# One relu per block of four groups, sums four groups behind, and a ring of 21 groups in a graph-network kernel

## The chip, the cores and the metric

The kernel runs on one core of one Trainium2 chip. The metric is the device time of one execution in microseconds (us), as the median of several runs; lower is better. A core has five engines that run side by side and meet through semaphores: TensorE (PE in the profile; PEld is its loading of weights), VectorE (DVE), ScalarE (ACT), GpSimd (POOL) and SyncE (SP). Transfers are done by 16 DMA engines; here SyncE issues the plain ones and GpSimd the gathers, one instruction for each 128 rows that are fetched by a list of indices.

## The reference

The task is one layer of a graph network over 12,500 nodes with 96 features and 412,500 edges, sorted by their target node, with 4 features each.

```python
def _mlp(h, W, b, gamma, beta):
    h = jax.nn.relu(h @ W + b)
    mu = jnp.mean(h, axis=0)
    var = jnp.mean(jnp.square(h - mu), axis=0)
    return gamma * (h - mu) * jax.lax.rsqrt(var + EPS) + beta

node_feat = _mlp(x, W_node, b_node, g_node, beta_node)
edge_feat = _mlp(edge_attr, W_edge, b_edge, g_edge, beta_edge)
message = jnp.concatenate([x[row], x[col], edge_feat], axis=1)
message = _mlp(message, W_msg, b_msg, g_msg, beta_msg)
agg = jax.ops.segment_sum(message, col, num_segments=N)
out = _layernorm(x + agg + node_feat)
```

The means and variances of an `_mlp` go over all rows, so over all edges for the messages. Everything is in float32.

## The kernel before

The message of an edge is relu(P[src] + Q[dst] + edge part), where P and Q are products of `x` with two thirds of `W_msg`. The first stages make the tables P and Q (`table`), the nodes' own part (`nodes`), and the statistics of the edges' part (`edge_norm`, L273). They end near 1045 us. Then comes the loop over the edges (`fast`, L327), which ends near 5317 us, and a last stage for the layer norm (L701 on).

**Tiles.** 128 edges make a tile, four tiles a group (512 edges), four groups a block (`BG`). There are 806 groups in 202 blocks. P's rows for a group are gathered by GpSimd, four gathers of 128 rows, into a place of the `ring` (L89), which has `RING` places. The groups of the first 26 blocks (`SPILL`) were gathered in the stages before and laid off in DRAM; SyncE brings such a block back as `pb`. `order` (L357) mixes these 26 blocks evenly among the 176 that are gathered while the loop runs. The first `RING` groups of the latter are gathered ahead of the loop (L353).

**One block.** `load` has SyncE fetch the edges' features and 31 rows of Q for each group. `edges` (L429) multiplies the edge features on TensorE into `pr`. `prepare` (L436) turns `pr` into `left`: ScalarE's relu (L440) for the edge part, and VectorE's comparison (L441) for 31 rows that pick the target node. `linear` (L443) multiplies `left` with `rhs` for one group into `z`, of which there are two buffers, so the product of group k+1 needs the addition of group k-1 to be done. `message` (L451) adds the gathered rows (`hs`, L463, VectorE), which frees the ring's place, and takes the relu into `h` (L465, ScalarE) for two groups at a time. Once per block it also writes an indicator of the target node into `h` (L457, VectorE). `sums` (L471) multiplies `h` with itself and the indicator on TensorE (L480), which gives sums by node and the moments for the statistics, in `pa`. `add` (L483) adds `pa` into `agg` (L493, two instructions) and `gram` (L494) on VectorE.

**Order.** In this loop the order of every engine's instructions is written out by hand: each engine does them in the order of the program. Step k of the loop (L506) issues the product of group k+1, the message of group k, and the sums of group k-2; in a block's first step also `edges` of the next block, in its third `prepare` of the next block; and `add` when `SKEW` steps have passed since the block's first. After the message of a gathered group the gathers for the group `RING` places further on are issued. `h` and `left` have two buffers, `rhs` three.

Of the kernel before, what the change touches and what calls it, by code (L numbers as in the profile page):

```python
# [11 lines left out]
F32 = mybir.dt.float32  # L12
I32 = mybir.dt.int32
AF = mybir.ActivationFunctionType
# [6 lines left out]
N, C, E, ED = 12500, 96, 412500, 4  # L21
EPS = 1e-5
P = 128
# [3 lines left out]
GT, GE, BG = 4, 512, 4  # L27
NT = -(-E // P)
NG = -(-NT // GT)
# [18 lines left out]
WN, WS, WM = 31, 16, 7  # L48
# [1 line left out]
KR = C + WN + 1  # L50

SPILL = 26 * BG
RING = 25
RAW = 3
SKEW = 6
HB, RB = 2, 3
CL, CE = 2, 2
J = 8
# [14 lines left out]
def gnn(ctx, tc, t):  # L73
    nc = tc.nc
# [13 lines left out]
    nc.sync.dma_start(src_raw, t["src"][:, :RAW * BG * GT])  # L88
    ring = rpool.enter_context(tc.tile_pool(name="ring", bufs=RING))  # L89
    xp = xpool.enter_context(tc.tile_pool(name="x", bufs=1)).tile([C, NN], F32, name="xp")  # L90
# [27 lines left out]
    rel = const.tile([P, NGP, GT], F32, name="rel")  # L118
# [71 lines left out]
    for i in range(NS):  # L190
        k, n = Q * i, C - Q * i
# [135 lines left out]
    def fast(ring):  # L327
        def ahead_of(g):
            return gather(g, ring.tile([P, GT, C], F32, name="pg"))

        with tc.manual_schedule(engines={ET.SP, ET.Pool}):
# [6 lines left out]
            for r in range(WM + NN, WT, 64):  # L338
                n = min(64, WT - r)
# [6 lines left out]
            n = 0  # L346
# [4 lines left out]
            for _ in store:  # L351
                pass
            got = {g: ahead_of(g) for g in range(SPILL, SPILL + RING)}  # L353

# [10 lines left out]
        with tc.tile_pool(name="fix", bufs=1) as fix, tc.tile_pool(name="msg", bufs=2) as work, \  # L365
# [12 lines left out]
            for x in hb:  # L378
                nc.vector.memset(x[:, :, :, C:C + 1], 1.0)

            eas, block, prs, zs, pas, pair = {}, {}, {}, {}, {}, [None]

            def load(s):

                b = order[s]
                first = SPILL // BG
                c, o = ((b - first) // CL * CL + first, CL) if b >= first else (b // CE * CE, CE)
                if c not in eas:
                    o = min(o, NBL - c)
                    eas[c] = work.tile([P, o, GE], F32, name="ea" if b >= first else "eae")  # L390
                    for i in range(BG):
                        nc.sync.dma_start(eas[c][Q * i:Q * i + EK, :, :], t["ea"][EK * i:EK * (i + 1), c:c + o, :])
                    nc.sync.dma_start(eas[c][EK:P:Q, :, :], rel_d[:, c * BG * GE:(c + o) * BG * GE]
                                      .rearrange("o (b g e) -> (o g) b e", g=BG, e=GE))
                ea = eas[c][:, b - c, :]
                _, val = nc.values_load_multi_w_load_instructions(
                    base[:, b:b + 1], engines=[ET.SP], min_val=0, max_val=N - 1,
                    skip_runtime_bounds_check_because="they are nodes' numbers")
                rows = q_tab[bass.ds(val[0], WN), :]
                rows = bass.AP(rows.tensor, rows.offset, [[C, WN], [WS * C, BG], [1, C]], None, rows.runtime_checks)  # L400
                nc.sync.dma_start(rhs[C:C + WN, s % RB, :, :], rows)
                block[s] = ea

            def fetch(s):
                b = order[s]
                if b * BG < SPILL:
                    back = work.tile([P, BG, GT, C], F32, name="pb")
                    nc.sync.dma_start(back, spill[b].rearrange("p g (a c) -> p g a c", a=GT))
                    for i in range(BG):
                        got[b * BG + i] = back[:, i, :, :]  # L410
# [18 lines left out]
            def edges(s):  # L429

                prs[s] = ps.tile([P, BG, GE], F32, name="pr", bufs=1)
                for i in range(min(BG, NG - order[s] * BG)):
                    nc.tensor.matmul(prs[s][:C + WN, i, :], we[Q * i:Q * i + EK + 1, :],  # L433
                                     block[s][Q * i:Q * i + EK + 1, :], start=True, stop=True)

            def prepare(s):  # L436

                n = min(BG, NG - order[s] * BG)
                pr, x = prs[s], left[s % 2]
                nc.scalar.activation(x[:C, :n, :], pr[:C, :n, :], AF.Relu)  # L440
                nc.vector.tensor_scalar(x[C:C + WN, :n, :], pr[C:C + WN, :n, :], 0.0, None, op0=OP.is_equal)  # L441

            def linear(k):  # L443
                s, g = steps[k]
                n = min(GT, NT - g * GT)
                zs[k] = ps.tile([P, GT, C], F32, name="z")
                for i in range(n):
                    nc.tensor.matmul(zs[k][:, i, :], left[s % 2][:KR, g % BG, i * P:(i + 1) * P],  # L448
                                     rhs[:KR, s % RB, g % BG, :], start=True, stop=True)

            def message(k):  # L451
                s, g = steps[k]
                n = min(GT, NT - g * GT)
                i = g % BG
                h, z, pg = hb[s % HB], zs.pop(k), got.pop(g)
                if i == 0:
                    nc.vector.tensor_tensor(  # L457
                        h[:, :, :, C + 1:C + 1 + WN], rel[:, g:g + BG, :].unsqueeze(3).to_broadcast([P, BG, GT, WN]),
                        iota.unsqueeze(2).to_broadcast([P, BG, GT, WN]), op=OP.is_equal)
                if i % 2 == 0:  # L460
                    pair[0] = work.tile([P, 2, GT, C], F32, name="hs")
                hs = pair[0]
                nc.vector.tensor_add(hs[:, i % 2, :n, :], z[:, :n, :], pg[:, :n, :])  # L463
                if i % 2 and n == GT:
                    nc.scalar.activation(h[:, i - 1:i + 1, :, :C], hs, AF.Relu)  # L465
                elif i % 2 or g == NG - 1:
                    for o in range(i // 2 * 2, i + 1):
                        m = GT if o < i else n
                        nc.scalar.activation(h[:, o, :m, :C], hs[:, o % 2, :m, :], AF.Relu)

            def sums(k):  # L471

                s, g = steps[k]
                n = min(GT, NT - g * GT)
                h = hb[s % HB][:, g % BG, :, :]
                if g % BG == 0:
                    pas[s] = ps.tile([C + 1, BG, P], F32, name="pa")
                for i in range(n):
                    r = min(P, E - (g * GT + i) * P)
                    nc.tensor.matmul(pas[s][:, g % BG, :C + 1 + WN], h[:r, i, :C + 1], h[:r, i, :C + 1 + WN],  # L480
                                     start=i == 0, stop=i == n - 1)
# [15 lines left out]

            n, ahead = len(steps), SPILL + RING
            with tc.manual_schedule(engines={ET.SP, ET.Pool, ET.PE, ET.DVE, ET.Activation}):
                load(0)  # L500
                fetch(0)
                load(1)
                edges(0)
                prepare(0)
                linear(0)
                for k in range(n + SKEW):  # L506
                    s, g = steps[min(k, n - 1)]
                    if k < n and g % BG == 0:
                        if s + 2 < len(order):
                            load(s + 2)  # L510
                        if s + 1 < len(order):
                            fetch(s + 1)
                    if k + 1 < n:
                        linear(k + 1)
                    if k < n:
                        message(k)
                    if 0 <= k - 2 < n:
                        sums(k - 2)
                    if k < n and s + 1 < len(order):
                        if g % BG == 0:  # L520
                            edges(s + 1)
                        if g % BG == 2:
                            prepare(s + 1)
                        if g % BG == 3 and order[s + 1] < RAW:
                            convert(s + 1)
                    if k >= SKEW and (k - SKEW) % BG == 0:
                        add((k - SKEW) // BG)
                    if k < n and g >= SPILL and ahead < NG:
                        got[ahead] = ahead_of(ahead)
                        ahead += 1  # L530
# [12 lines left out]
    def general():  # L543

        with tc.tile_pool(name="gd", bufs=1, space=DRAM) as gd, tc.tile_pool(name="gfix", bufs=1) as fix, \
# [138 lines left out]
            for b in range(NB):  # L684
# [7 lines left out]
                nc.vector.tensor_copy(agg[:, WM + b * P:WM + (b + 1) * P], px)  # L692

    fast(ring)
    rpool.close()
    bad = nc.values_load(flag, min_val=0, max_val=1, skip_runtime_bounds_check_because="a comparison's result")
# [4 lines left out]
    with tc.tile_pool(name="fin", bufs=2) as work, tc.tile_pool(name="fin_ps", bufs=2, space=PSUM) as ps:  # L701
# [10 lines left out]
        for i in range(0, NB, NBY):  # L712
            n = min(NBY, NB - i)
# [55 lines left out]
```

## Time and profile before

| | |
|---|---|
| median of 3 runs | 5365.72 us (5353.82 to 5367.68) |
| the profiled execution | 5379.39 us, with a span of 5377.6 us |
| loop over groups | about 1045 to 5317 us |
| TensorE, weight load, VectorE, ScalarE, GpSimd busy | 3364.1, 2570.3, 1699.3, 1077.6, 3106.6 us |
| granted TensorE clock, mean of the span | 0.665 of full speed |
| gathers in the loop's ring | 2807, of 959 ns each |
| `hs` addition, relu of two groups, L457, L441 | 555, 843, 666 and 2291 ns each |

A row of a group reads: line, engine, operation, what it writes and reads, and after the bar its time in all and the mean of one in ns. A row of the timeline reads: start and duration in us, engine, line, operation, what it writes and reads, how many were merged, and in brackets how long the engine stood idle before and what ended that. "Issue" stands for time in which the engine waited for nothing that the profile shows, "remote" for a signal whose sender it cannot name. A row of the stretches gives the busy time of each engine, with the number of instructions, the granted TensorE clock as a share of full speed, the share of the DMA engines' time, and GB/s.

### The profile page before, as it was taken

The numbers are of one execution on the slowest core, as the hardware profiler recorded it, in microseconds if no ns is written. First come the engines' busy times: TensorE is split into PE (matmuls) and PEld (weight loads), VectorE is DVE, ScalarE is ACT, GpSimd is POOL, SyncE is SP. The second block draws the span as 40 slices with busy tenths as digits, with TensorE's granted clock in tenths as the row PEclk, the third lists the DMA queues.
The fourth block names the chain that finished last, engine by engine and source line by source line (L and its number), as shares of the span: only waits on it lengthen the run. The fifth ranks groups of instructions, "written<-read, shape, count | busy, mean of one in ns | idle before, by whom it ended". The sixth has DMA issues, their size and how long they took to land. (4 is left out here: it accounts for less than half of the span.)

```text
span 5377.6 us, 46715 instructions
## 1 busy us (share of the span) xinstructions
PE 3364.1 (63%) x16705; PEld 2570.3 (48%) x16705; DVE 1699.3 (32%) x2622; ACT 1077.6 (20%) x1015; POOL 3106.6 (58%) x3244
## 2 busy tenths in 40 slices
PE   5566662666656666665667666656666666666668
PEld 5333330354545545544445554544455545545447
DVE  1445551622222322222222322322232222223225
ACT  0224441411111111111111111111111111111112
POOL 5454456155566656666666666666666666666661
PEclk9755555566666766667676766666766666666667
DMA  5332332111111111111111111111111111111112
GB/s 165 112 97 61 71 68 48 29 33 37 39 44 38 43 42 44 43 38 42 42 43 45 42 38 43 44 42 45 37 43 42 41 45 36 43 43 42 44 37 84
DMA packets 188578, 270.80 MB, mean 50 GB/s; under 512 B 121095, under 2 KB 121480, under 8 KB 187330
## 3 DMA queue, kind: packets, MB, share of 16 engines
q0 software_dynamic: 103136, 158.62, 12.2%
q1 hardware_dynamic: 77120, 98.40, 6.6%
q10 hardware_dynamic: 8080, 10.71, 0.7%
q8 instruction: 133, 2.18, 0.2%
q14 instruction: 109, 0.89, 0.1%
HBM read 225.90 MB, written 41.60 MB: 50 GB/s over the span
## 5 line engine op out<-in xcount | busy, mean ns | idle before, releaser
L162 POOL DMA_INDIRECT pg<-p_tab,src x2807 | 2690.8, 959 | 1767.1 <-DVE hs L463 922.8
L448 PE MATMUL z<-rhs,left 128*128 128x96 f32 x6446 | 1222.7, 339 | 878.3 <-issue 672.8
L448 PEld LDWEIGHTS z<-rhs,left 128*128 128x128 f32 x6446 | 1093.2, 249 | 1183.6 <-issue 903.1
L480 PE MATMUL pa<-h 128*97 128x128 f32 x6446 | 1246.3, 331 | 556.2 <-issue 551.6
L480 PEld LDWEIGHTS pa<-h 128*97 128x97 f32 x6446 | 1015.4, 209 | 654.7 <-issue 653.3
L463 DVE TENSOR_TENSOR hs<-z,pg 128x384 f32<-128x384 f32 x702 | 385.2, 555 | 2599.2 <-remote 1537.6
L465 ACT ACTIVATE h<-hs 128x768 f32<-128x768 f32 x402 | 338.9, 843 | 2867.6 <-DVE hs L463 1846.0
L290 PE MATMUL pr<-ea,wide 10*128 10x512 f32 x1212 | 405.4, 1074 | 285.7 <-issue 177.6
L162 POOL DMA_INDIRECT stage<-p_tab,src x368 | 351.0, 954 | 369.6 <-DMA spill<-stage 240.0
L440 ACT ACTIVATE left<-pr 96x2048 f32<-96x2048 f32 x202 | 377.2, 1867 | 643.6 <-remote 439.7
L441 DVE TENSOR_SCALAR left<-pr 31x2048 f32<-31x2048 f32 x202 | 462.9, 2291 | 108.3 <-ACT left L440 75.5
L296 DVE BATCH_NORM_STATS2 estats<-r 128x6 f32<-128x512 f32 x606 | 365.8, 678 | 326.8 <-issue 191.1
L433 PE MATMUL pr<-ea,we 6*127 6x512 f32 x1404 | 411.1, 808 | 62.6 <-issue 47.5
L290 PEld LDWEIGHTS pr<-ea,wide 10*128 10x128 f32 x1212 | 209.6, 320 | 480.2 <-issue 291.8
L294 ACT ACTIVATE r<-pr 128x1024 f32<-128x1024 f32 x303 | 297.1, 1024 | 458.0 <-remote 290.0
L433 PEld LDWEIGHTS pr<-ea,we 6*127 6x127 f32 x1404 | 117.9, 223 | 206.6 <-issue 190.6
L457 DVE TENSOR_TENSOR h<-rel,iota 128x496 f32<-128x496 f32 x202 | 134.6, 666 | 0.0
L463 DVE TENSOR_TENSOR hs<-z,pb 128x384 f32<-128x384 f32 x104 | 56.6, 554 | 233.1 <-remote 85.2
L150 PE MATMUL pt<-w_msg,xp 96*128 96x96 f32 x392 | 88.7, 421 | 60.4 <-issue 37.1
L493 DVE TENSOR_TENSOR agg<-pa,agg 97x62 f32 x404 | 90.1, 223 | 85.4 <-remote 54.8
L150 PEld LDWEIGHTS pt<-w_msg,xp 96*128 96x128 f32 x392 | 85.5, 330 | 63.4 <-issue 48.6
L494 DVE TENSOR_TENSOR gram<-pa,gram 97x388 f32<-97x388 f32 x202 | 111.4, 551 | 0.1
(107 smaller groups left out, 634.7 us busy)
## 6 DMA issues: line engine op xcount, KB each, us to landing
pg<-p_tab,src POOLq DMA_INDIRECT x2807
spill<-stage SPq DMA_DIRECT2D x26, 768.0 KB
pb<-spill SPq DMA_DIRECT2D x26, 768.0 KB
ea<-in_ea SPq DMA_DIRECT2D x75, 160.0 KB
rhs<-q_tab SPq DMA_DIRECT2D x202, 46.5 KB
ea<-in_ea SPq DMA_DIRECT2D x352, 20.0 KB
stage<-p_tab,src POOLq DMA_INDIRECT x368
q_tab<-trow SPq DMA_DIRECT2D x7, 672.0 KB
```

Of the source, the lines that this page charges most:

```text
L150: nc.tensor.matmul(pt[:, g, :], xp[:, k:k + P], w, start=True, stop=True)
L162: nc.gpsimd.indirect_dma_start(out=pg[:, i, :], out_offset=None, in_=tab[:, :], in_offset=bass.IndirectOffsetOnAxis(ap=idx[:, k:k + 1], ax ...
L290: nc.tensor.matmul(pr[:, k % 2, :], wide[Q * i:Q * i + 2 * EK, :], ea[Q * i:Q * i + 2 * EK, b % J, :], start=True, stop=True)
L294: nc.scalar.activation(r, pr, AF.Relu)
L296: nc.vector.bn_stats(stats[:, (k - o) % NS, (k - o) // NS, :], r[:, 1 - o, :])
L433: nc.tensor.matmul(prs[s][:C + WN, i, :], we[Q * i:Q * i + EK + 1, :], block[s][Q * i:Q * i + EK + 1, :], start=True, stop=True)
L440: nc.scalar.activation(x[:C, :n, :], pr[:C, :n, :], AF.Relu)
L441: nc.vector.tensor_scalar(x[C:C + WN, :n, :], pr[C:C + WN, :n, :], 0.0, None, op0=OP.is_equal)
L448: nc.tensor.matmul(zs[k][:, i, :], left[s % 2][:KR, g % BG, i * P:(i + 1) * P], rhs[:KR, s % RB, g % BG, :], start=True, stop=True)
L463: nc.vector.tensor_add(hs[:, i % 2, :n, :], z[:, :n, :], pg[:, :n, :])
L465: nc.scalar.activation(h[:, i - 1:i + 1, :, :C], hs, AF.Relu)
L480: nc.tensor.matmul(pas[s][:, g % BG, :C + 1 + WN], h[:r, i, :C + 1], h[:r, i, :C + 1 + WN], start=i == 0, stop=i == n - 1)
```

## The change

The relu of a block's four groups becomes one ScalarE instruction, issued after the fourth addition; its buffer `hs` now holds four groups, twice. The sums of a group are issued four steps behind its message in place of two (`BG` for 2), and `add` eight steps after a block's first in place of six. The indicator (L457) is written after the third addition of a block, ahead of the next block's `prepare`, and no longer ahead of the first. The ring has 21 places in place of 25, which gives back the memory that `hs` takes.

```diff
--- before.py
+++ after.py
@@ -50,9 +50,9 @@
 KR = C + WN + 1
 
 SPILL = 26 * BG
-RING = 25
+RING = 21
 RAW = 3
-SKEW = 6
+SKEW = 8
 HB, RB = 2, 3
 CL, CE = 2, 2
 J = 8
@@ -378,7 +378,7 @@
             for x in hb:
                 nc.vector.memset(x[:, :, :, C:C + 1], 1.0)
 
-            eas, block, prs, zs, pas, pair = {}, {}, {}, {}, {}, [None]
+            eas, block, prs, zs, pas, four = {}, {}, {}, {}, {}, [None]
 
             def load(s):
 
@@ -454,19 +454,20 @@
                 i = g % BG
                 h, z, pg = hb[s % HB], zs.pop(k), got.pop(g)
                 if i == 0:
+                    four[0] = work.tile([P, BG, GT, C], F32, name="hs")
+                hs = four[0]
+                nc.vector.tensor_add(hs[:, i, :n, :], z[:, :n, :], pg[:, :n, :])
+                if i == min(2, NG - 1 - (g - i)):
+                    b = g - i
                     nc.vector.tensor_tensor(
-                        h[:, :, :, C + 1:C + 1 + WN], rel[:, g:g + BG, :].unsqueeze(3).to_broadcast([P, BG, GT, WN]),
+                        h[:, :, :, C + 1:C + 1 + WN], rel[:, b:b + BG, :].unsqueeze(3).to_broadcast([P, BG, GT, WN]),
                         iota.unsqueeze(2).to_broadcast([P, BG, GT, WN]), op=OP.is_equal)
-                if i % 2 == 0:
-                    pair[0] = work.tile([P, 2, GT, C], F32, name="hs")
-                hs = pair[0]
-                nc.vector.tensor_add(hs[:, i % 2, :n, :], z[:, :n, :], pg[:, :n, :])
-                if i % 2 and n == GT:
-                    nc.scalar.activation(h[:, i - 1:i + 1, :, :C], hs, AF.Relu)
-                elif i % 2 or g == NG - 1:
-                    for o in range(i // 2 * 2, i + 1):
+                if i == BG - 1 and n == GT:
+                    nc.scalar.activation(h[:, :, :, :C], hs, AF.Relu)
+                elif i == BG - 1 or g == NG - 1:
+                    for o in range(i + 1):
                         m = GT if o < i else n
-                        nc.scalar.activation(h[:, o, :m, :C], hs[:, o % 2, :m, :], AF.Relu)
+                        nc.scalar.activation(h[:, o, :m, :C], hs[:, o, :m, :], AF.Relu)
 
             def sums(k):
 
@@ -514,8 +515,8 @@
                         linear(k + 1)
                     if k < n:
                         message(k)
-                    if 0 <= k - 2 < n:
-                        sums(k - 2)
+                    if 0 <= k - BG < n:
+                        sums(k - BG)
                     if k < n and s + 1 < len(order):
                         if g % BG == 0:
                             edges(s + 1)
```

## The prediction

> **What bounds the kernel now.** I read the page first, then the busy time by stretch, then the list of waits, then some 20 us of the timeline in order of time. The page says that no engine is full:
>
> ```profile
> PE 3364.1 (63%) x16705; PEld 2570.3 (48%) x16705; DVE 1699.3 (32%) x2622; ACT 1077.6 (20%) x1015; POOL 3106.6 (58%) x3244
> ```
>
> PE is TensorE, DVE VectorE, ACT ScalarE, POOL GpSimd. The change lies in the loop over groups, which runs from about 1045 us to 5317 us of the 5377.6 us span. The stretches of that loop (columns: PE, PEld, DVE, ACT, POOL busy, granted TensorE clock, DMA share, GB/s):
>
> ```profile
> 2100.00:3100.00 1000.00, 648.88 (x3396) 508.33 (x3396) 277.44 (x423) 166.72 (x141) 625.72 (x654) 0.69 0.16 42
> 3100.00:4100.00 1000.00, 626.59 (x3348) 496.39 (x3348) 275.78 (x419) 165.84 (x140) 627.85 (x655) 0.68 0.17 42
> 4100.00:5100.00 1000.00, 641.48 (x3370) 510.51 (x3370) 275.09 (x420) 166.50 (x141) 622.36 (x648) 0.67 0.16 42
> 5246.00:5317.00 71.00, 62.86 (x503) 55.91 (x501) 40.73 (x66) 24.19 (x22) 1.50 (x2) 0.93 0.07 21
> ```
>
> In the last row GpSimd has no gathers left, and the rest goes through at 503 matmuls in 71 us (7.1 per us, clock 0.93) against 3.4 per us before. So the chip can run this loop at twice its pace, and does not while gathers stream. The waits (us in total, times, longest) say who stands:
>
> ```profile
> ACT h L465 <- DVE hs L463: 1846.0, 222, 25.0
> DVE hs L463 <- remote: 1622.8, 186, 16.4
> POOL pg L162 <- DVE hs L463: 922.8, 167, 131.2
> PEld z L448 <- issue: 903.1, 650, 10.4
> PEld pa L480 <- issue: 653.3, 710, 2.6
> ```
>
> GpSimd waits for `hs`, the VectorE addition that frees a place of the ring; VectorE waits for a signal that the view cannot name. ScalarE's wait is idle time and costs nothing by itself. The sums (`pa`, L480) wait for "issue" and not once in the list for ScalarE's relu. The timeline shows the round:
>
> ```profile
> 3002.23 1.03 PE L448 MATMUL z<-rhs,left 128*128 128x96 f32 x8
> ...
> 3023.12 0.32 PE L448 MATMUL z<-rhs,left 128*128 128x96 f32 x1 [1.08 <-issue]
> ...
> 3026.86 0.56 DVE L463 TENSOR_TENSOR hs<-z,pg 128x384 f32<-128x384 f32 x1 [9.47 <-remote]
> ...
> 3027.69 0.94 POOL L162 DMA_INDIRECT pg<-p_tab,src  x1 [4.59 <-DVE hs L463]
> ...
> 3028.68 2.30 DVE L441 TENSOR_SCALAR left<-pr 31x2048 f32<-31x2048 f32 x1 [1.26 <-ACT left L440]
> ...
> 3031.00 0.48 DVE L493 TENSOR_TENSOR agg<-pa,agg 97x62 f32 x2
> ...
> 3031.07 1.99 PE L448 MATMUL z<-rhs,left 128*128 128x96 f32 x8 [2.00 <-issue]
> 3031.40 0.55 DVE L494 TENSOR_TENSOR gram<-pa,gram 97x388 f32<-97x388 f32 x1
> ...
> 3031.87 0.55 DVE L463 TENSOR_TENSOR hs<-z,pg 128x384 f32<-128x384 f32 x1
> 3032.33 0.67 DVE L457 TENSOR_TENSOR h<-rel,iota 128x496 f32<-128x496 f32 x1
> ```
>
> At 3002 TensorE does eight matmuls in 1.03 us; at 3023 it crawls, one instruction per 0.70 us, while GpSimd issues a gather each 1.25 us. GpSimd then fills the ring and pauses (last gather issued at 3022, next at 3027.69); some 3 us into the pause TensorE runs again. Counted over the trace, GpSimd pauses 206 times between 1100 and 5240 us, 1018 us in sum, about once per block, and TensorE does about 144 instructions (a block's worth) from one restart to the next. In the pauses the crawl is gone after 3.5 us. So the loop is a round: four groups' gathers (20 us, or less when spilled blocks pass), then a pause that ends when the next `hs` comes. I don't know why TensorE crawls; its rule is read off the trace. What TensorE waits for at its own pace is seen at 3031.07: the first product of a block starts 0.1 us after VectorE's L441 has ended. Counted, the first product of a block follows L441 within 0.3 us in 135 of 188 blocks; the second one is held by the `hs` of the previous block's last group in 56 of 195 blocks; no other product is held often.
>
> **The change part by part.** Steps are named by the position i of a group in its block (0 to 3).
>
> *Relu.* Two ACTIVATEs of 843 ns per block (L465, 128x768) become one of 128x1536. ScalarE's L440 reads 2048 per partition in 1867 ns, so (1867-843)/(2048-768) = 0.80 ns per element, and the new one takes 0.843 + 768 x 0.80 ns = 1.46 us by estimate (that slope is of a PSUM source). Saved: 0.23 us x 201 = 46 us of ScalarE time. It is worth 0, since ScalarE is busy 166 us in 1000. The end of a block's relu moves from 0.56+0.84 to 0.56+1.46 us after the last addition starts. Cover: between the last addition and the first sum that needs it TensorE does product, sum, product (lag of four), 3 x 0.87 = 2.6 us at full clock against 2.0 and about 0.2 of signals. 0, with 0.4 us to spare; without that cover 0.62 x 201 = 125 us.
>
> *Sums four groups behind.* TensorE's instructions and the places of products and `edges` stay the same. No wait on relu is in the list, so nothing is removed: 0. The loop drains two steps longer, with the same work: +2 us, bounds 0 and 5 (two groups at 2.5).
>
> *Ring of 21.* In every round the ring is full: counted, GpSimd is never less than 22.75 groups ahead until its gathers run out. In the loop depth is worth 0. But 25 groups are gathered before the loop while GpSimd stands idle up to 131.2 us; 4 of them now move into the loop. And at the end 28 groups pass in 71 us, 2.54 each, against 742 additions in the 4000 us from 1100 to 5100, 5.39 each: four groups go from the quick end into the loop, 4 x 2.85 = +11 us. Bounds: 0, and 16 gathers x 1.25 = 20 us.
>
> *L457 (the indicator, 0.67 us) moves* from ahead of addition 0 to between addition 2 and L441. L441 is what the next block's first product waits for. Where L441 was waiting for ScalarE's L440 (72 of 188 blocks started over 0.1 us after addition 2), L457 fits into that gap; the mean delay of L441, worked out block by block, is 0.46 us, or 0.32 if L440, no longer queued behind the relu of groups 0 and 1 (21 of 188 blocks), starts earlier. Taken 0.40 us x 145 blocks (72% of 202) = 58 us if all of it is paid. Nothing is paid if GpSimd's 20 us cover it: TensorE crawls later at 0.70 us per instruction, so 0.4 us earlier in the round are less than one instruction. I take half, +29. Bounds 0 and 0.67 x 202 = 135. Behind L457 stand L441 and addition 3; it waits itself for sums that lie ahead of the product of addition 2, so it adds no wait. SP's loads and GpSimd's gathers keep their places in their own queues.
>
> *Agg and gram (2 x 0.223 + 0.551 = 1.00 us) move* from behind L441 at i = 2 to behind addition 0. Addition 3 therefore comes 1.00 - 0.46 = 0.54 us earlier. It held the second product in 56 of 195 blocks, 58 of 202: -31 us if all is gained, 0 if late signals hold it. I take -16. They now stand ahead of addition 1: nothing waits for that addition soon (19 blocks held there, 5.7 us), so 0; but 24 of the pauses of GpSimd end with it, bound 24 x 1.0 = 24 us. Agg waits for the last sum of its block, which TensorE issues ahead of addition 1's product.
>
> Sum: 0 + 2 + 11 + 29 - 16 = +26 us. The profiled execution took 5379.39 us, so 5405 on its scale; it lies 13.7 us above the median of 5365.72, so **5392 us** on the median's scale, +0.5%. A change within 0.3% (16 us) is about what a measurement cannot tell from none.
>
> [...]
>
> **The rivals.**
>
> *Faster: VectorE's new order wins.* Place: between L441 and addition 3. If L441's delay is wholly covered by the gathers and addition 3's gain is paid in full (1.00 us x 58 = -58), and L440 starts up to 0.84 us earlier in 22 blocks (-18), the time is 5366 + 13 - 76 = 5303 us; half of it gives 5340. For it: the waits "DVE hs <- remote" of 1622.8 us show that additions are what GpSimd waits for. Against: these are late signals, which no order on VectorE mends. It decides where addition 3 brings GpSimd's restart forward in more than some 20 blocks by 1 us.
>
> *No change.* The pauses alone set the time; the skew does not do anything, as it removes a wait that is not in the list; what is left is the ring and the drain, 5366 + 13 = 5379 us. For it: 144 instructions per round whatever the pace. Against: 135 blocks where TensorE stands for L441.
>
> *Much slower: relu of four groups comes late.* The 0.4 us to spare is worked out from full clock; if signals take longer than that, TensorE stands 0.62 us at a block's first sum: 5392 + 125 = 5517 us. For it: in the trace signals come late by many us. Against: at half clock the cover is twice as long. It decides once the first sum of a block starts right behind relu in over half of the blocks.
>
> **How the numbers follow.** Slightly slower as summed 0.46 (its own range 5375 to 5440), faster 0.28, no change 0.18, much slower 0.08. The summed case has some part, 0.03, inside 0.3%. The range that leaves out under 2 in 10 goes from the full gain of the first rival to most of the bound of L441's delay (5379 + 100): 5305 to 5480 us. Faster 0.28, same 0.21, slower 0.51.
>
> **What would show it.** Right: relu near 1.46 us x201; GpSimd's pauses still about 200 and its last gather within some 60 us of the loop's end; the first product of a block right behind L441 in at least 7 of 10 blocks, and L441 right behind L457. Wrong: fewer or shorter pauses (then the round has another length than a block), sums waiting for relu, or a crawl with another budget than 144 instructions. The weakest point is that I take the crawl as given; if what triggers it depends on the order of the sums, the sign can be either.

## The result

The changed kernel takes 5338.50 us in the median of 10 runs (5330.86 to 5356.62). The kernel before, in 10 runs beside them, takes 5357.87 us (5348.50 to 5371.96; the 5365.72 us of the first part were three of these). The ratio is 0.9967 with a 95% interval of 0.9952 to 0.9982: faster by 0.33%, or 18 us (10 to 26). The forecast was 5392 us, slower. Its range of 5305 to 5480 us holds the time; its sign is wrong.

The profiled execution of the changed kernel took 5331.84 us, with a span of 5330.1 us. It is 47.5 us shorter than the one of the kernel before, but only 19 us separate the medians: one profile came from a quick execution and the other from a long one. Any reading of the pair has to allow for some 20 us in each.

The busy times of the changed kernel, from the top of its page:

```profile
PE 3244.9 (61%) x16705; PEld 2513.6 (47%) x16705; DVE 1710.2 (32%) x2622; ACT 1037.7 (19%) x814; POOL 3111.7 (58%) x3244
```

ScalarE has 201 instructions fewer (814 for 1015) and 39.9 us less work; the others do what they did. The stretches of the loop in the changed kernel (busy time of PE, PEld, DVE, ACT and POOL with the number of instructions, granted TensorE clock, DMA share, GB/s); the last row has almost no gathers:

```profile
2100.00:3100.00 1000.00, 613.79 (x3342) 490.14 (x3341) 275.95 (x419) 156.27 (x93) 623.24 (x652) 0.68 0.18 42
3100.00:4100.00 1000.00, 621.90 (x3396) 496.02 (x3395) 284.86 (x427) 157.76 (x94) 633.31 (x658) 0.69 0.18 42
4100.00:5100.00 1000.00, 611.91 (x3386) 495.54 (x3385) 280.48 (x424) 157.76 (x94) 630.09 (x657) 0.69 0.18 42
5200.00:5275.00 75.00, 63.58 (x489) 54.83 (x487) 40.72 (x75) 21.63 (x15) 6.82 (x8) 0.91 0.08 24
```

The three middle stretches hold 10,124 matmuls, those of the kernel before 10,114. So the loop runs at the same pace to 0.1%, and GpSimd issues 1967 instructions in them against 1957. The last row is still twice as quick as the rest. The waits of the changed kernel (us in total, times, longest):

```profile
DVE hs L459 <- remote: 1738.3, 187, 16.3
ACT left L440 <- remote: 1388.5, 77, 25.5
PEld z L448 <- issue: 1193.4, 736, 11.1
PE z L448 <- issue: 974.4, 569, 10.8
POOL pg L162 <- DVE hs L459: 804.3, 132, 131.1
...
ACT h L466 <- DVE hs L459: 704.6, 125, 15.8
```

The same waits lead the list in another order. ScalarE's wait for the additions has shrunk (1846.0 to 704.6 us, as it now asks once per block), and its wait ahead of L440 has grown (439.7 to 1388.5). TensorE's weight loads for the products stand 290 us longer (903.1 to 1193.4) and yet the time is shorter. That is the first sign that this wait is not what sets the time. The timeline of one block shows the new order on VectorE:

```profile
3030.07 0.56 DVE L459 TENSOR_TENSOR hs<-z,pg 128x384 f32<-128x384 f32 x1 [12.14 <-remote]
...
3030.55 0.67 DVE L462 TENSOR_TENSOR h<-rel,iota 128x496 f32<-128x496 f32 x1
3030.90 1.13 POOL L162 DMA_INDIRECT pg<-p_tab,src  x1 [3.49 <-DVE hs L459]
3031.25 2.30 DVE L441 TENSOR_SCALAR left<-pr 31x2048 f32<-31x2048 f32 x1
...
3033.57 0.56 DVE L459 TENSOR_TENSOR hs<-z,pg 128x384 f32<-128x384 f32 x1
...
3033.64 2.00 PE L448 MATMUL z<-rhs,left 128*128 128x96 f32 x8 [4.50 <-issue]
...
3034.22 1.48 ACT L466 ACTIVATE h<-hs 128x1536 f32<-128x1536 f32 x1 [3.67 <-DVE hs L459]
...
3037.38 0.48 DVE L494 TENSOR_TENSOR agg<-pa,agg 97x62 f32 x2 [1.15 <-issue]
3037.78 0.55 DVE L495 TENSOR_TENSOR gram<-pa,gram 97x388 f32<-97x388 f32 x1
```

Addition 2, the indicator (L462), L441 and addition 3 follow each other without a gap; the next block's first product starts 0.09 us after L441 ends. One relu of 1.48 us follows, and agg and gram come behind addition 0 of the next block. GpSimd restarts with addition 2, as in a round of before, and does not see the rest.

Each profile was then split in stages (us, worked out from the traces): up to the first L296 of the edge statistics, from there to the last L296, and the loop from its first to its last addition. Some 40 us between the last two and 64 or 65 after them are left out.

| kernel | ahead of edge statistics | edge statistics | loop | span |
|---|---|---|---|---|
| before | 315.0 | 690.6 | 4268.6 | 5377.6 |
| changed | 294.7 | 673.1 | 4257.3 | 5330.1 |

Of the 47.5 us, 20.3 lie ahead of the edge statistics, where the two kernels have the same code: that is scatter between executions (294.7 to 315.0 us in all ten profiles with the long times of this kind). 17.5 lie in the edge statistics, which the change does not touch either, but in which the gathers for the ring run. 11.3 lie in the loop. The prediction had nothing in the second stage.

### The profile page after: what moved, and what is told of

Same layout as the page of the kernel before. It is cut to its first block, busy times and chain, and to the rows that moved or that the text cites. A ratio compares the mean times of both kernels' runs of the same rounds, so it can differ in the third digit from the quotient of the medians.

```text
span 5330.1 us, 46323 instructions
## 1 busy us (share of the span) xinstructions
PE 3244.9 (61%) x16705; PEld 2513.6 (47%) x16705; DVE 1710.2 (32%) x2622; ACT 1037.7 (19%) x814; POOL 3111.7 (58%) x3244
## 5 line engine op out<-in xcount | busy, mean ns | idle before, releaser
L448 PE MATMUL z<-rhs,left 128*128 128x96 f32 x6446 | 1200.8, 334 | 989.3 <-issue 974.4
L448 PEld LDWEIGHTS z<-rhs,left 128*128 128x128 f32 x6446 | 1075.7, 245 | 1275.3 <-issue 1193.4
L481 PE MATMUL pa<-h 128*97 128x128 f32 x6446 | 1233.9, 329 | 575.5 <-issue 563.9
L481 PEld LDWEIGHTS pa<-h 128*97 128x97 f32 x6446 | 1002.0, 207 | 679.5 <-issue 667.2
L440 ACT ACTIVATE left<-pr 96x2048 f32<-96x2048 f32 x202 | 377.6, 1869 | 2424.0 <-remote 1388.5
L466 ACT ACTIVATE h<-hs 128x1536 f32<-128x1536 f32 x201 | 298.1, 1483 | 1137.3 <-DVE hs L459 704.6
L441 DVE TENSOR_SCALAR left<-pr 31x2048 f32<-31x2048 f32 x202 | 462.8, 2291 | 57.2 <-ACT left L440 52.6
L296 DVE BATCH_NORM_STATS2 estats<-r 128x6 f32<-128x512 f32 x606 | 365.2, 678 | 309.9 <-issue 177.1
L433 PE MATMUL pr<-ea,we 6*127 6x512 f32 x1404 | 337.3, 765 | 50.7 <-issue 38.4
L433 PEld LDWEIGHTS pr<-ea,we 6*127 6x127 f32 x1404 | 97.6, 213 | 153.6 <-issue 134.2
L462 DVE TENSOR_TENSOR h<-rel,iota 128x496 f32<-128x496 f32 x202 | 134.4, 666 | 0.0
```

The costliest lines, as they stand in the source:

```text
L296: nc.vector.bn_stats(stats[:, (k - o) % NS, (k - o) // NS, :], r[:, 1 - o, :])
L466: nc.scalar.activation(h[:, :, :, :C], hs, AF.Relu)
```

## The experiments

Two theories stood after this comparison. The first: the gathers ahead of the loop are not free, the edge statistics slow down while they run, and the smaller ring pays there what it loses in the loop. The second, that of the first part: the ring costs 11 us, and the order on VectorE, with GpSimd's restart earlier, brings what was gained. All ratios below are to the kernel before on the same chip, with 95% intervals.

### Ring of 21 alone, and the order of agg and gram alone

The kernel before with one edit:

```diff
-RING = 25
+RING = 21
```

> The kernel before with RING = 21 alone. Ring theory: every group gathered ahead of the loop slows the edge statistics by about 4.4 us (their stage took 690.6 us with 25 groups and 673.1 us with 21 in the two traces) and saves 2.85 us at the loop's end, so 4 x (2.85 - 4.4) = -6 us, between -4 and -10; the stage itself 17 us shorter. Order theory (VectorE's new order made all of the gain, and gathers ahead of the loop are hidden): +11 us as in the prediction, and the stage before the loop as long as before.

And with two, which moves agg and gram behind addition 0 and leaves relu, indicator and sums as they were:

```diff
-RING = 25
+RING = 21
-SKEW = 6
+SKEW = 8
```

> The kernel before with RING = 21 and SKEW = 8: only the additions into agg and gram move, from behind L441 to behind a block's first addition. Theory that the gain comes from addition 3 no longer queued behind them: 1.0 us for some 58 blocks, so 30 to 58 us below the run with RING = 21 alone. Rival, that late signals hold addition 3 anyway: within 8 us of RING = 21 alone.

Measured in five rounds beside the kernel before at 5350.13 us: the ring alone 5352.97 us, 1.0000 [0.9985, 1.0014]; with agg and gram moved 5342.50 us, 0.9981 [0.9973, 0.9990]. The ring is worth 0, within 8 us, which leaves out the second theory's +11 and not the first's -6. The move is worth -10 us, within 9: less than the 30 to 58 of the one forecast, and about the 8 that the other allowed. The rest of the change (relu, sums, indicator) is the difference from 0.9981 to 0.9967, -7 us within 9, and the two ratios were measured apart: not told from nothing.

What the move does to TensorE is much larger than what it does to the time. TensorE's mean idle time before a product, by the position of its block (us, worked out from the traces):

| kernel | first | second | third | fourth | per block |
|---|---|---|---|---|---|
| before | 2.43 | 1.12 | 0.72 | 0.12 | 4.39 |
| ring of 21 | 2.50 | 0.91 | 0.72 | 0.13 | 4.26 |
| ring of 21, agg and gram moved | 2.02 | 0.42 | 0.69 | 0.22 | 3.34 |
| changed | 3.01 | 0.56 | 0.65 | 0.17 | 4.39 |

The move takes 0.92 us per block off these waits, 186 us over 202 blocks, and 10 us off the time. By the reading of the round in the timeline, TensorE arrives earlier at a point where it then crawls at 0.70 us per instruction, until GpSimd's pause ends the crawl; no run tests that reading by itself.

### A ring of 9

A size far outside, so that a price per group can be read: the kernel before and the changed kernel with

```diff
-RING = 25
+RING = 9
```

(in the changed kernel the line taken out is `RING = 21`).

> The kernel before with RING = 9. Ring theory: sixteen groups fewer ahead of the loop, 16 x (2.85 - 4.4) = -25 us, the stage of the edge statistics about 70 us shorter, and no more waits for gathers in the loop since the ring was always full. Rival: a ring of 9 runs empty when TensorE is quick, and the loop grows by over 50 us; prediction's own term: +46 us.

> The changed kernel with RING = 9. Ring theory: 12 groups fewer than its 21, 12 x (2.85 - 4.4) = -19 us against it, so about 38 us below the kernel before (ratio 0.993). If the ring does nothing: ratio 0.9967 as for the changed kernel. If depth is needed: slower than the changed kernel.

Measured on the same chip as the two kernels above: the kernel before with 9 groups 5325.75 us, 0.9955 [0.9939, 0.9972], the changed kernel with 9 groups 5328.86 us, 0.9954 [0.9937, 0.9970]. A ring of 9 is 24 us faster than one of 25, as the first theory had it (-25). With 9 groups the rest of the change brings nothing (+3 us, within 12), so the 0.993 expected of the changed kernel did not come. The edge statistics in the kernel before, in that with a ring of 21 and that with 9, as the view of line L296 gives them (durations, first and last start):

```profile
L296 DVE BATCH_NORM_STATS2 estats<-r x606: 635/676/696, 315.0 to 1005.6; 128x6 f32<-128x512 f32 x152
```

```profile
L296 DVE BATCH_NORM_STATS2 estats<-r x606: 635/676/696, 294.7 to 966.5; 128x6 f32<-128x512 f32 x152
```

```profile
L296 DVE BATCH_NORM_STATS2 estats<-r x606: 635/676/696, 294.9 to 907.9; 128x6 f32<-128x512 f32 x152
```

The median of one instruction is 676 ns in all three; the stage takes 690.6, 671.8 and 613.0 us. That is (690.6 - 671.8) / 4 = 4.7 us per group gathered ahead, and (671.8 - 613.0) / 12 = 4.9 us; a group's four gathers take 4 x 1.25 = 5.0 us on GpSimd. The other profiles of this kind with the same ring agree: 699.4 us with 25 groups; 673.1, 669.2 and 673.1 us with 21; 612.0 us with 9. So a group gathered ahead of the loop costs nearly the time of its gathers there, in a stage that needs nothing of it. The windows of the kernel before show the place:

```profile
700.00:800.00 100.00, 64.32 (x196) 34.67 (x192) 58.06 (x97) 46.06 (x48) 52.97 (x56) 0.50 0.32 71
800.00:900.00 100.00, 18.69 (x36) 4.52 (x36) 11.58 (x18) 9.22 (x9) 75.65 (x80) 0.50 0.22 52
900.00:1000.00 100.00, 69.12 (x224) 39.05 (x224) 71.04 (x119) 59.52 (x60) 11.35 (x12) 0.50 0.15 31
```

While GpSimd issues 80 gathers without a pause (800 to 900 us), TensorE does 36 matmuls and ScalarE 9 instructions; with 12 gathers in the next 100 us it is 224 and 60. In the loop the groups that are not gathered ahead cost (4297.4 - 4260.8) / 12 = 3.1 us each (the loops of the rings of 9 and 21), close to the 2.85 us of the prediction; the changed kernel's two loops (4257.3 and 4304.1) give 3.9, and all of these are single profiles. With 3.1 a smaller ring wins some 1.8 us per group: 12 x 1.8 = 22 us from 21 to 9, measured 27 within 12, and 7 us from 25 to 21, measured 0 within 8.

### Another chip: the crawl is not everywhere

The next four kernels ran on a chip on which the kernel before takes 4172.87 us, not 5350. The edits, each to the changed kernel except the last. The indicator behind L441 and addition 3, next to its old place ahead of the next block's addition 0:

```diff
-                if i == min(2, NG - 1 - (g - i)):
+                if i == min(3, NG - 1 - (g - i)):
```

> The changed kernel with the indicator (0.67 us on VectorE) written after addition 3 in place of addition 2, so behind L441 and no longer ahead of it. Both theories: TensorE's mean gap before a block's first product, 3.01 us in the changed kernel's trace, falls by about 0.5 us. Theory that the round of gathers covers TensorE's waits: the time stays within 10 us of the changed kernel's (ratio 0.995 to 0.9985). Rival, that L441's delay was paid as the prediction took it: 29 to 100 us faster than the changed kernel (ratio 0.991 or less).

Relu by pairs again, with all else as changed:

```diff
-                if i == BG - 1 and n == GT:
-                    nc.scalar.activation(h[:, :, :, :C], hs, AF.Relu)
+                if i % 2 and n == GT:
+                    nc.scalar.activation(h[:, i - 1:i + 1, :, :C], hs[:, i - 1:i + 1], AF.Relu)
...
```

> The changed kernel with relu for two groups at a time again; sums still four groups behind, indicator, agg and gram and ring as in the change. Theory that ScalarE is off the path: same as the changed kernel, ratio 0.995 to 0.9985. Rival, that the larger relu made what the moved agg and gram (0.9981 with the smaller ring) did not: back to 0.998 or more.

The ring's groups gathered one after each spilled block from the start of the edge statistics on. The four gathers of a group follow the 16 of the block without a gap, so GpSimd pauses after streams of mostly 20 or 40 gathers (25 or 50 us, with pauses of 17 to 30 us behind them in the trace from a crawling chip below):

```diff
...
+                    g = SPILL + len(got)
+                    if g < SPILL + RING:
+                        got[g] = ahead_of(g)
...
```

> The changed kernel, with one group of the ring gathered after each spilled block from the start of the edge statistics on, where GpSimd has pauses, in place of all 21 in one go at their end. Theory that only gathers without a pause make the engines crawl: the edge statistics, 673 us in the changed kernel's trace, fall by 50 to 90 us, and the time with them (ratio 0.98 to 0.988). Rival, that a gathered group costs about 4.9 us there wherever it is put: no change against the changed kernel.

And the kernel before without the gathers inside the loop; the additions read the rows of the first ring places again and again, so that part of the computation is left out:

```diff
+            kept = [got[g] for g in range(SPILL, SPILL + RING)]
...
-                        got[ahead] = ahead_of(ahead)
+                        got[ahead] = kept[ahead % RING]
```

> The kernel before without the gathers inside the loop: each group there adds rows that were gathered ahead of the loop for another group, so the output is not the reference's. If gathers cause TensorE's steps of 0.70 us: these are gone from the loop, and its 806 groups pass at about the pace of the last 28 before (2.5 us), 2.1 ms in place of 4.27. Rival, that the steps come from TensorE's own instruction stream: they stay, and the loop takes over 3 ms.

Measured: indicator behind L441 4147.07 us, 0.9939 [0.9926, 0.9953]; relu by pairs 4159.98 us, 0.9976 [0.9967, 0.9985]; paced gathers 4261.73 us, 1.0216 [1.0202, 1.0230]; without gathers 2640.12 us in one run. The expectations speak of a chip like the one before and fall with it. On this chip the loop has no crawl: steps of 0.65 to 0.75 us from one TensorE instruction (product or weight load) to the next make up 3 to 8 us of a loop with gathers here, and 783 us in the first profile of the kernel before. The next chip (kernel before 4165.54 us) was of the same kind. The changed kernel itself was run there, and a ring of 9 with the indicator behind L441 (both edits are shown above):

> The changed kernel itself, beside the kernel before. On a chip whose engines crawl while gathers stream (before near 5350 us): ratio 0.9967 again, TensorE's gaps before a block's products 4.4 us in sum as before. On a chip without the crawl (before near 4173 us): the gathers' pace alone sets the end, so the ring and the skew do nothing, and only what lies on GpSimd's path counts: ratio between that with relu by pairs (0.9976) and that with the indicator behind L441 (0.9939).

> The changed kernel with the indicator behind L441 and RING = 9. On a chip with the crawl: 12 groups fewer ahead of the loop, 10 to 25 us faster than the changed kernel. On a chip without it: the 84 gathers ahead of the loop there run up to the loop's start without costing the edge statistics anything, so with 36 GpSimd stands idle for some 48 us before the loop, and the time is 40 to 50 us longer than with RING = 21 (ratio 1.004 to 1.007).

Measured: the changed kernel 4159.52 us beside 4165.54, 0.9985 [0.9976, 0.9994]; with 9 groups and the indicator behind L441 4197.23 us, 1.0081 [1.0067, 1.0096]. On such a chip gathers cost the edge statistics next to nothing: from 400 to 500 us of the changed kernel's profile there, 80 gathers run beside 339 matmuls, and VectorE is busy all the time. The stage is as long with 21 groups (244.1 to 614.4 us) as with 9 (242.9 to 611.9), though this by itself says little, as only 42 and 36 of the ring's gathers fall into it. There the deep ring pays: the smaller one leaves GpSimd idle for 48 us ahead of the loop. The loss is 44 us by the spans of the two profiles with the indicator behind L441 (4146.2 and 4190.6) and 59 us by their ratios (1.0081 - 0.9939), but these come from two chips; so it lies at the expected 40 to 50 us or above.

I call the two kinds crawling chips (kernel before 5350 to 5412 us; three met, and that of the first result, which may be one of them) and free chips (4164 to 4173 us, three met). What makes a chip one or the other was not found. One of the 15 executions of the kernel before on the second free chip took 5180.12 us, at a granted clock of 1.00; it has no trace, so that the kind belongs to the chip alone is not shown. The first result is from a crawling chip.

### The crawl and the gathers, on a crawling chip

The kernel before once more, and the kernel without the loop's gathers (the edit shown above, with the same part left out), on one crawling chip:

> The kernel before, unchanged, for a second profile. On a chip with the crawl: span near 5350 us, TensorE's steps of 0.70 us some 1000 us of the loop, edge statistics near 690 us. On a chip without it: span near 4170 us, edge statistics near 369 us, GpSimd hardly idle in the loop; if gathers set the end there, the mean time from gather to gather is 1.258 to 1.260 us (the changed kernel had 1.257, and each 0.001 us is 2.7 us of the time).

> The kernel before without the gathers inside the loop (each group adds rows gathered ahead of the loop for another group), as in the earlier run without gathers, which met no crawl even beside the kernel before. On a chip with the crawl: if streaming gathers cause it, the loop takes 1.9 to 2.1 ms as on the other chip; if the crawl is the chip's whatever is run, well over 3 ms.

The kernel before took 5404.78 us, the one without gathers 3032.20 us. One window of the first:

```profile
2000.00:2950.00 950.00, 586.90 (x3155) 468.22 (x3156) 259.95 (x396) 154.07 (x131) 592.92 (x619) 0.68 0.18 42
```

and the same of the second:

```profile
2000.00:2950.00 950.00, 869.56 (x7388) 757.34 (x7386) 598.11 (x921) 365.70 (x308) 0.00 (x0) 1.00 0.08 22
```

Without gathers there are 7388 matmuls in 950 us against 3155, the clock is 1.00 against 0.68, and not one step of 0.70 us is left. The loop takes 1912.7 us, as on the free chip (1916.9). The crawl needs the gathers: that is shown. Why uninterrupted gathers slow TensorE's instructions is not.

### Indicator and pacing, on a crawling chip

The two edits of the changed kernel that had met a free chip, again:

> The changed kernel with the indicator behind L441, once more, for a chip with the crawl. If the round of gathers covers TensorE's waits: TensorE's gap before a block's first product shrinks by about 0.5 us x 202 = 100 us, and the time stays within 10 us of the changed kernel's (ratio 0.995 to 0.9985). If L441's delay is paid: 29 to 100 us faster than the changed kernel (0.991 or less). On a chip without the crawl: 0.994 again.

> The changed kernel with a group of the ring gathered after each spilled block, once more, for a chip with the crawl. If only gathers without a pause make the engines crawl: edge statistics of 673 us fall by 50 to 90 us, ratio 0.98 to 0.988. If a gathered group costs about 4.9 us wherever it is put: within 10 us of the changed kernel. On a chip without the crawl: 1.02 again, since the spilled blocks then come later and the edge statistics wait for them.

Measured beside 5353.03 us: indicator behind L441 5344.65 us, 0.9983 [0.9966, 0.9999]; paced gathers 5345.84 us, 0.9986 [0.9969, 1.0003]. The first product's mean wait falls from 3.01 to 2.08 us and the second's from 0.56 to 0.42, over 1 us per block, some 200 us in sum, and the time does not fall (changed: 0.9967). The indicator ahead of L441 costs nothing that can be measured on a crawling chip.

The pacing was expected to bring 50 to 90 us and brought none. The edge statistics took 665.0 us in place of 673.1. A gathered group costs the stage about the same in either place. That a pause does not help is not shown by this: the four gathers of a group lengthen the stream of a spilled block from 16 gathers to 20, and in the loop the crawl sets in some 12 us after a stream starts (median of 136 rounds of the first profile), well within either. On the free chip the paced order made the stage 472 us long in place of 369, which is why it lost 2.2% there.

### The parts, on a free chip

The four kernels that split the change, in five rounds beside 4163.78 us:

> The changed kernel once more. With the crawl: 0.9952 to 0.9982 again. Without: 0.9976 to 0.9994.

> The kernel before with RING = 21 alone, once more. Order theory: 1.000 with the crawl. Ring theory: 4 x (2.85 - 4.9) = -8 us with the crawl, ratio 0.9985. Without the crawl: 1.000, since only 74 or so of the gathers ahead of the loop are done when it starts, whatever the ring.

> RING = 21 and agg and gram behind a block's first addition, once more. Order theory with the crawl: 8 us or more below the ring alone. Ring theory: within 6 us of it. Without the crawl: within 4 us of the kernel before.

> The changed kernel with relu by pairs, for a chip with the crawl. If the relu of four does nothing: within 6 us of the changed kernel. If the fewer instructions of ScalarE help: 8 us or more above it. Without the crawl: 0.9976 again.

| kernel | us | ratio | interval |
|---|---|---|---|
| ring of 21 alone | 4165.94 | 1.0004 | 0.9995 to 1.0013 |
| ring of 21, agg and gram moved | 4138.80 | 0.9944 | 0.9930 to 0.9957 |
| changed, relu by pairs | 4157.06 | 0.9985 | 0.9976 to 0.9994 |
| changed | 4158.08 | 0.9988 | 0.9979 to 0.9997 |

Here the intervals separate the parts. Moving agg and gram brings 25 us; within 4 had been expected. The rest of the change gives 18 of them back, and the indicator's place accounts for it as far as ratios from two free chips can be set side by side: with it behind L441 the changed kernel stood at 0.9939. The relu of four groups is worth 0 (within 6 us). What sets the pace on a free chip can be seen in the changed kernel's page, waits and one stretch of its loop:

```profile
PE 2731.3 (66%) x16705; PEld 2306.4 (56%) x16705; DVE 1712.9 (41%) x2622; ACT 1041.9 (25%) x814; POOL 3091.2 (74%) x3244
```

```profile
DVE hs L459 <- DMA pg<-p_tab,src: 1815.9, 449, 9.0
...
POOL pg L162 <- issue: 760.9, 2497, 0.3
```

```profile
700.00:800.00 100.00, 87.28 (x702) 76.14 (x700) 54.30 (x85) 32.59 (x22) 75.85 (x80) 0.95 0.24 57
```

The additions wait for gathered rows; GpSimd waits for nobody (0.3 us between two gathers, 80 in 100 us), and while it issues them TensorE does 702 matmuls in 100 us, at the clock of 0.95. Gathers end to end are the bound. Their groups (count, busy us, mean ns) with the ring alone and with agg and gram moved:

```profile
L162 POOL DMA_INDIRECT pg<-p_tab,src x2807 | 2682.5, 956 | 856.5 <-issue 768.8
```

```profile
L162 POOL DMA_INDIRECT pg<-p_tab,src x2807 | 2659.8, 948 | 855.8 <-issue 766.5
```

8 ns less per gather, 22.7 us over 2807 of them: that is the loop's gain of 23.7 us (3446.8 to 3423.1). Which gathers are long was counted over the loops: with the ring alone 113 of the 261 gathers that run beside the indicator take over 0.96 us, in the changed kernel 102 of 260, but 42 of 278 with agg and gram moved and 38 of 271 in the changed kernel with the indicator behind L441. Beyond 945 ns each, the gathers beside the indicator sum to 33.2 us with the ring alone and 10.9 with agg and gram moved, which is nearly the whole difference.

What decides is when the gather starts. In these four traces every gather that starts with 200 to 700 ns of the indicator still to come is long (266 of 266), and none that starts in its last 100 ns is (0 of 135). Beside L441, with the ring alone, none of 495 is long. Of the gathers that run already when the indicator starts, 3 of 614 are. The order on VectorE moves these starts: 54 and 56 gathers fall into the last 100 ns in the two quick kernels, 12 and 13 in the two others. So a gather that starts under the indicator is held up, and the order decides how often that happens; why the indicator holds it is not shown.

## Why the prediction was wrong

**Ring of 21 (+11): failed, and the sign with it.** Its size in the loop was near (3.1 to 3.9 us per group between rings of 9 and 21; 2.85 by the step). What failed is the sentence that the groups ahead of the loop are gathered "while GpSimd stands idle": GpSimd's idle time is not the price, the edge statistics' is, at 4.4 to 4.9 us per group. The window from 800 to 900 us of the kernel before, with 36 matmuls beside 80 gathers, was there to be read; I read the loop alone. The step measured 0 within 8 us, with 17 us less in the edge statistics and the loop's loss against it. That loss cannot be seen in the single profiles of 25 and 21 groups, whose loops scatter by 20 us.

**The indicator ahead of L441 (+29): failed.** The delay is there: L441 now starts 0.80 us after addition 2 in the mean (0.46 before), and the first product follows L441 within 0.3 us in 89% of the blocks (72%). It is not paid. With the indicator put behind L441 again, the time stands at 0.9983 against 0.9967: no gain in that order, and the difference of the two ratios is -0.0016 within 0.0023, which leaves out a price of 29 us (0.0054), as far as ratios measured on two chips can be set side by side. The step took half between "paid" and "covered by GpSimd's 20 us"; the right end was "covered", for which it had the argument itself (0.4 us earlier is less than one crawled instruction). With these two terms at nothing, the prediction's sum of +26 would have been -14 us, and 18 us less were measured.

**Agg and gram (-16): right sign, mechanism and size near.** Measured -10 within 9. Again only a small part of what TensorE gains is paid: 186 us of idle time, 10 us of time. That half of -31 comes near is partly luck, since the half was a choice between two ends.

**Relu (0): right.** 1483 ns for the estimated 1.46 us, as the group of the changed kernel shows:

```profile
L466 ACT ACTIVATE h<-hs 128x1536 f32<-128x1536 f32 x201 | 298.1, 1483 | 1137.3 <-DVE hs L459 704.6
```

The cover for the later relu was nearly enough: the waits list has 19 waits of the sums for it, 11.5 us in sum and at most 0.6 us each, far from the half of the blocks that the rival "much slower" needed. **Sums four behind (+2): right** within what can be measured; the work after the last gather took 53.6 us for 24 groups, 67.1 for 28 before, 2.2 and 2.4 each.

**The longer first gap.** The first product's mean gap grew from 2.43 to 3.01 us. The granted clock over the span did not fall with it (0.665 before, 0.672 changed). In the kernel before, eight matmuls of L448 took 1.03 us at 3002 us, at a granted clock of 1.00, and 1.99 us at 3031 us, at 0.50.

**The rivals.** "VectorE's new order wins", at half its gain 5340 us, has the measured time by luck: it counts the ring as +11. Its first condition (L441's delay covered) is shown. Its second, addition 3 paid in full, is not: the gain was some 10 us of 58. The 58 was too much from the start, since the indicator stands ahead of addition 3 in any case and leaves it 0.54 us of the 1.00, as the prediction's own step has it (31 us). Where the 18 us come from stays open in part. Ring 0 within 8, agg and gram -10 within 9, the rest -7 within 9 add up to it, but the rest is a difference of ratios measured apart, and it and the move could each be near zero or twice as large; with a ring of 9 the changed order brings nothing (within 12).

**The signs named beforehand** came out as for the slower case, but for those 19 waits: relu near 1.46 us x201, GpSimd's pauses 202 (counted as in the prediction), its last gather 53.6 us ahead of the loop's last addition, L441 right behind the indicator, the first product right behind L441 in 9 of 10 blocks. The count of pauses was loose: 206 with 1018 us does not come out of the idle time of GpSimd between gathers, which is 806 us in 187 stretches of over 0.4 us (changed: 783 in 189). The signs tested the mechanism of the waits and not whether a wait is paid, and so could not warn of the sign.

No version is the best on both kinds of chip. The ring of 9 is the fastest on crawling chips (0.9955) and lost 0.8% on free ones, where it was tried together with the indicator behind L441. The changed kernel with the indicator behind L441 (0.9939 and 0.9983) and the kernel before with a ring of 21 and agg and gram moved (0.9944 and 0.9981) are faster than the kernel before on both, and faster than the change on free chips; on crawling ones they cannot be told from it.

## What to carry to other kernels

Before a wait is priced, ask who paces the loop and whether that engine ever waits for the one that stands: here 186 us of TensorE's idle time went for 10 us. Work done ahead of a loop is free only if the stage that it runs in says so; compare that stage's pace with and without it, engine by engine. What a part is worth differs by chip too (agg and gram moved: 0.9981 on a crawling one, 0.9944 on a free one): run the parts beside the kernel before on one chip, and if the times there are far from the known ones, read the profile anew before using the old reasons.

## What the chips showed that was not expected

- The same kernel takes 5350 to 5412 us on some chips and 4164 to 4173 us on three others, 28% apart. On the slower ones TensorE's instructions step 0.70 us apart: in the first profile of the kernel before from some 12 us after GpSimd's gathers set in (about 130 TensorE instructions) until some 3 us into its next pause: 783 us of a loop of 4269 in steps of 0.65 to 0.75 us. VectorE and ScalarE show no step of 0.68 to 0.72 us in that loop. Without the loop's gathers the steps are gone from it, and the loop takes 1913 us on a crawling chip and 1917 on a free one.
- Whether the crawl comes from the fetching of instructions, no run here shows. The 133 transfers of 16 KB in the profile's instruction queue take as long on a crawling chip (1.06 us in the mean of the first profile) as on a free one (1.10 us in the last profile of the changed kernel). So these transfers are not slower there; whether they come late was not measured.
- A group gathered ahead costs a crawling chip 4.4 to 4.9 us in the stage beside it. On a free chip the stage took 369 us with 9 groups and 370 with 21, and a ring that is too small costs 4 to 5 us per group.
- VectorE's indicator (666 ns) lengthens a gather that starts while 200 to 700 ns of it are still to come, in 266 of 266 cases in four traces of free chips, and in 0 of 135 where less than 100 ns are left. There the order on VectorE decides how many gathers are hit: 113 of 261 beside it, or 38 of 271.
